# A per-sample term carried in eight extra contraction rows instead of an opening product, with label gathers of eight row counts at the start

## The chip, the cores and the metric

The kernel runs on one core of a Trainium2 chip. The metric is the time of one execution on the device, in microseconds. A run of a kernel beside the kernel before, on one chip, is called a session here. Within a session the executions of one kernel agree to about 0.5%; between sessions they need not, and much of this document is about that. The records of every execution also give the span of the core and the mean clock granted to TensorE. The automatic state label of an execution compares it only with others of the same kernel in its session, so it reads "fast" for everything below; "quick session" and "slow session" are words of this document, defined by the time of the kernel before in that session (11.2 ms or 15.4 to 15.7 ms).

## The reference

For 16,384 samples with 69 items and one label each, rows of an embedding table (96 values) are fetched, combined, weighted by a small network, pooled into ten groups, and passed through a three-layer top.

```python
u = emb[batch_user]                              # 16384 x 69 x 96
ql = emb[batch_label[:, 0]]                      # 16384 x 96
q = jnp.broadcast_to(ql[:, None, :], u.shape)
z = jnp.concatenate([q, u, q - u, q * u], axis=-1)
h = _dice(z @ W1 + b1, a1, EPS_DICE)             # "first product"
att = (h @ W2 + b2) @ W3 + b3
pre = jnp.where((batch_user < ITEM_NUM)[..., None], u * att, 0.0)
pooled = jnp.einsum('gf,bfe->bge', window, pre)
# ... three dense layers on [pooled, ql]
```

Split by the four parts of z, `z @ W1 + b1` is `u (W1b - W1c) + (q*u) W1d + c`, with `c = q (W1a + W1c) + b1`. The term c is the same for all 69 items of a sample. The change is about how c gets into the sum.

## The kernel before

The samples go in 32 blocks of 512, a block in 69 chunks of 512 items, and two chunks make a "pair", the step of the main loop. A main chunk holds 8 samples with 64 items each; the 5 remaining items of each sample make 5 tail chunks. Per chunk GpSimd issues four gathers of 128 rows, TensorE transposes them, ScalarE and VectorE copy them out as `uT` and `quT`, and the first product accumulates two parts in a PSUM bank:

```python
def seed(i):                                  # opens the bank of a pair with c
    ph = ps_h.tile([P, 512], F32, tag="h", ...)
    nc.tensor.matmul(ph, zrow[:, 0:P], zrow, start=True, stop=False)   # zeros, bf16
    ...
    nc.scalar.copy(ph.rearrange("h (s f) -> h s f", f=FM),
                   by_field(cs[n0][0][:, k0 * NS : (k0 + 1) * NS]))    # c, per sample
def hidden(i, ph, uT, quT):
    for w, x, last in [(A, uT, False), (Wp, quT, True)]:
        for j in range(2):
            nc.tensor.matmul(ph[j * H1 : (j + 1) * H1, :], w, x[:, j, :], start=False, stop=last)
```

The label rows of a block are needed once, at its head, and come two ways. The first block's are gathered by GpSimd. Those of the other 31 blocks are loaded one row at a time on the SyncE queue, 512 rows a block, each with its row number in a register:

```python
for i, row in enumerate(at):                  # 32 rows per step of the main loop
    nc.sync.dma_start(out=qs[n][p + i : p + i + 1, k, :], in_=emb[bass.ds(row, 1), :])
...
for part in range(BLK // NLD):                # 16 steps, from 31 pairs before the block
    at(first - 31 + part, lambda n=n, part=part: head_gather(n, part))
at(first - 11, lambda n=n: head_turn(n, qs.pop(n)))      # transpose them
```

## Time and profile before

| kernel before | value |
|---|---|
| timed runs, median of 3 | 15,685.73 us (15,658.17 to 15,687.8) |
| the profiled execution | 11,178.86 us, clock 0.707 |
| TensorE / GpSimd / ScalarE / VectorE busy | 87% / 75% / 34% / 29% |
| gathers | 8832, one per 1.256 us |

```profile
1272.55 0.24 SPq L449 DMA_DIRECT2D out<-res  x1
1278.32 120.70 SPq L260 DMA_DIRECT2D q<-in_emb  x224
...
1404.58 156.49 SPq L260 DMA_DIRECT2D q<-in_emb  x288
1613.10 0.23 SPq L449 DMA_DIRECT2D out<-res  x1
```

The queue then stands still until the result of an earlier block is there to be sent; a view of its waits says the same (us in total, times, longest).

A block of the main loop lasts 342 us. So the queue is at work for over 80% of the time even in a quick session, and what it waits for is the progress of the rest.

### The profile page before, as it was taken

To read this page: it belongs to the slowest core of one execution; us is meant where nothing else is said; L and a number is where in the kernel's file an instruction comes from. 1 tells how busy PE (TensorE), PEld (TensorE's weight loads), DVE (VectorE), ACT (ScalarE), POOL (GpSimd) and SP (SyncE) were. 2 spreads that over 40 slices of the span, in tenths; PEclk is the share of its full clock that TensorE was granted. 3 is DMA by queue.
4 is the path that set the end of the run, shared out by engine and by line. 5 is a ranking of instruction groups with operands and counts; after the bars stand their busy time and mean duration, and the time that the engine had idled before them with its cause. 6 is when DMAs were issued, how large, how long until landed. Compare 5 with 4: busy or idle time off the path is not lost.

```text
span 11177.1 us, 157529 instructions
## 1 busy us (share of the span) xinstructions
PE 9700.5 (87%) x41348; PEld 4721.0 (42%) x41348; DVE 3187.3 (29%) x5424; ACT 3760.0 (34%) x6086; POOL 8404.8 (75%) x8842
## 2 busy tenths in 40 slices
PE   6888888888888898888888888888888888988888
PEld 3444444444444444444444444444444344444444
DVE  2222222222222222222222222222222222222222
ACT  2333333333333333333333333333333333333332
POOL 7777777777777777777777777777777777777775
PEclk6767677677776767767777667776677776677767
DMA  2222222222222222222222222222222222222221
GB/s 45 41 41 41 41 41 41 41 41 41 41 41 41 41 41 41 41 42 41 41 41 41 41 41 41 40 41 42 41 41 41 41 42 41 41 41 41 41 40 29
DMA packets 323169, 456.81 MB, mean 41 GB/s; under 512 B 175712, under 2 KB 180864, under 8 KB 322272
## 3 DMA queue, kind: packets, MB, share of 16 engines
q0 software_dynamic: 282752, 434.87, 19.6%
q1 hardware_dynamic: 37886, 10.92, 0.5%
q8 instruction: 333, 5.46, 0.2%
q14 instruction: 564, 4.62, 0.1%
q10 hardware_dynamic: 1634, 0.94, 0.0%
HBM read 446.04 MB, written 0.07 MB: 40 GB/s over the span
## 4 chain that ended last, share of the span: by engine, by line
PE 33%; POOL 32%; issue 16%; DMA 10%; SPq 5%; ACT 2%; DVE 1%; POOLq 0%; ACTq 0%
POOL u L229 32%; PE ph L343 12%; DMA u<-in_emb,rows 10%; PE acc L393 9%; PE p L423 4%; SPq L260 3%; PE ptr L325 3%; PE prow L354 2%; SPq L252 2%; PE ph L295 2%; PE pa L363 1%; ACT y L346 1%; DVE y L347 1%; ACT y L345 1%; PE patt L370 1%
## 5 line engine op out<-in xcount | busy, mean ns | idle before, releaser
L229 POOL DMA_INDIRECT u<-in_emb,rows x8832 | 8400.1, 951 | 2692.9 <-issue 2459.0
L325 PE MATMUL ptr<-ident,u 128*96 128x128 f32 x8832 | 2006.4, 353 | 1189.5 <-DMA u<-in_emb,rows 1172.1
L325 PEld LDWEIGHTS ptr<-ident,u 128*96 128x96 f32 x8832 | 1221.0, 155 | 3053.7 <-DMA u<-in_emb,rows 1526.9
L393 PEld LDWEIGHTS acc<-rw,u 128*96 128x96 f32 x16384 | 2048.5, 217 | 531.8 <-issue 531.2
L393 PE MATMUL acc<-rw,u 128*96 128x20 f32 x16384 | 2160.4, 282 | 1.8 <-DVE rw L376 1.3
L336 ACT COPY uT<-ptr 96x512 f32<-96x512 f32 x2208 | 1283.4, 581 | 2207.0 <-DVE quT L328 2039.4
L347 DVE TENSOR_TENSOR y<-ph,y 128x512 f32<-128x512 f32 x1104 | 763.5, 692 | 4394.8 <-ACT y L346 4292.3
L345 ACT ACTIVATE y<-ph 128x512 f32<-128x512 f32 x1104 | 659.1, 597 | 3754.1 <-PE ph L343 3753.9
L343 PE MATMUL ph<-uT,A 96*64 96x512 f32 x4416 | 1793.5, 904 | 0.0
L343 PE MATMUL ph<-quT,w 96*64 96x512 f32 x4416 | 1671.9, 847 | 0.0
L328 DVE TENSOR_TENSOR quT<-ptr,qT 96x512 f32<-96x512 f32 x2048 | 1348.9, 679 | 611.5 <-PE ptr L325 607.0
L402 DVE COPY pooled<-acc 96x160 f32<-96x160 f32 x1008 | 433.3, 430 | 2189.9 <-PE acc L393 2184.4
L346 ACT ACTIVATE y<-y,a1c,na1c 128x512 f32<-128x512 f32 x1104 | 897.2, 813 | 36.6
L343 PEld LDWEIGHTS ph<-quT,w 96*64 96x64 f32 x4416 | 442.8, 194 | 1074.9 <-issue 1074.9
L298 ACT COPY ph<-cT 128x512 f32<-128x512 f32 x1008 | 591.3, 587 | 498.2 <-PE ph L295 497.8
L295 PE MATMUL ph<-zrow 1*128 1x512 bf16 x1104 | 527.6, 478 | 193.4 <-DVE y L347 191.7
L423 PE MATMUL p<-pooled,wf 96*100 96x512 f32 x1280 | 659.4, 660 | 1.2 <-DVE x L427 0.8
L343 PEld LDWEIGHTS ph<-uT,A 96*64 96x64 f32 x4416 | 282.6, 177 | 550.0 <-issue 464.8
L354 PE MATMUL prow<-y,v 128*32 128x512 f32 x2208 | 455.2, 909 | 0.0
L356 ACT COPY row<-prow 128x512 f32<-128x512 f32 x276 | 161.5, 585 | 628.4 <-PE prow L354 622.9
L423 PEld LDWEIGHTS p<-pooled,wf 96*100 96x100 f32 x1280 | 232.2, 190 | 287.7 <-issue 285.5
L423 PE MATMUL p<-pre,V 96*100 96x512 f32 x640 | 314.6, 625 | 0.0
(71 smaller groups left out, 2318.5 us busy)
## 6 DMA issues: line engine op xcount, KB each, us to landing
q<-in_emb SPq DMA_DIRECT2D x15872, 0.4 KB
u<-in_emb,rows POOLq DMA_INDIRECT x8832
ids<-in_idx SPq DMA_DIRECT2D x32, 140.0 KB
wf<-in_Wf ACTq DMA_DIRECT2D x1, 825.0 KB
out<-res SPq DMA_DIRECT2D x32, 2.0 KB
w<-in_W SPq DMA_DIRECT2D x1, 96.0 KB
q<-in_emb,ids POOLq DMA_INDIRECT x4
wf<-in_Wf ACTq DMA_DIRECT2D x1, 62.5 KB
```

The lines of the kernel that those rows point to most:

```text
L229: nc.gpsimd.indirect_dma_start(out=dst, out_offset=None, in_=emb, in_offset=bass.IndirectOffsetOnAxis(ap=index, axis=0),)
L295: nc.tensor.matmul(ph, zrow[:, 0:P], zrow, start=True, stop=False)
L325: nc.tensor.transpose(ptr[:, t * P : (t + 1) * P], u[:, 4 * j + t, :], ident)
L328: nc.vector.tensor_tensor(quT[:, j, :].rearrange("e (s f) -> e s f", f=FM), ptr.rearrange("e (s f) -> e s f", f=FM), by_field(q[:, k * NS ...
L336: nc.scalar.copy(uT[:, j, :], ptr)
L343: nc.tensor.matmul(ph[j * H1 : (j + 1) * H1, :], w, x[:, j, :], start=False, stop=last)
L345: nc.scalar.activation(y, ph, AF.Sigmoid, scale=S_DICE)
L346: nc.scalar.activation(y, y, AF.Identity, bias=a1c, scale=na1c)
L347: nc.vector.tensor_mul(y, ph, y)
L354: nc.tensor.matmul(pr[32 * k : 32 * (k + 1), :], v2, y, start=True, stop=True)
L393: nc.tensor.matmul(pa[:, j, 2 * t : 2 * t + 2, :].rearrange("e n g -> e (n g)"), u[:, 4 * j + t, :], rw[:, i % 4, j, t, :], start=True, st ...
L423: nc.tensor.matmul(p1, w[:, h * DH : (h + 1) * DH], x, start=(k == 0), stop=(k == KTOP - 1))
```

## The change

Its intent: drop the opening product and ScalarE's copy of c. The stationary matrix A gets eight more rows, the c of the chunk's 8 samples, and the moving matrix `uT` gets eight constant rows that pick the sample of each column. Then the first product's contraction over 104 rows adds c by itself. As A now holds c, there are two halves of A for a block (32 chunks each), refilled by small transfers. In addition the first block's label tiles are each gathered with two smaller row counts before the full 128.

```diff
@@ constants
-    A = const.tile([E, H1], F32, name="A")
-    nc.vector.tensor_sub(A, w1[:, 1, :], w1[:, 2, :])
+    A = [const.tile([E + NS, HM, H1], F32, name=f"A{h}") for h in range(2)]
+    ...
+    uTs = [const.tile([E + NS, 2, 512], F32, name=f"uT{i}") for i in range(5)]   # rows 96.. one-hot by sample
@@ first_head
-        for k in range(NQ):
-            gather(q[:, k, :], ids[0][:, NT + k : NT + k + 1])
+        for k, part in enumerate([(127, 126), (125, 124), (122, 120), (119, 112)]):
+            for m in (*part, P):
+                gather(q[0:m, k, :], ids[0][0:m, NT + k : NT + k + 1])
@@ head_row and seed go; in their place
+    def head_rows(n):
+        c = bpool.tile([P, NQ, H1], F32, tag="c", name=f"c{n}")
+        pc = ps_x.tile([P, NQ, H1], F32, tag="x", name=f"pc{n}")
+        for k in range(NQ):
+            nc.tensor.matmul(pc[:, k, :], qTs[n % 2][:, k * P : (k + 1) * P], Cq, start=True, stop=True)
+        nc.scalar.copy(c, pc)
+        return c
+    def head_weights(c, h):
+        for s in range(NS):
+            for k in range(NQ // 2):
+                nc.sync.dma_start(
+                    out=A[h][E + s : E + s + 1, k * HM // 2 : (k + 1) * HM // 2, :],
+                    in_=c[s::NS, h * NQ // 2 + k, :],
+                )
@@ hidden
+                nc.tensor.matmul(p, A[k // HM][:, k % HM, :], uT[:, j, :], start=True, stop=False)
@@ plan of a block
+            at(first - 7, lambda n=n: head_weights(cs[n], 0))
+            at(first + 4, lambda n=n: head_weights(cs.pop(n), 1))
```

Left out: bookkeeping, the tail chunks (which take c from a product of their own with Cq), and smaller buffer edits.

More of the change, by code (lines that the diff above doesn't have):

```diff
@@ L31 @@
 F32 = mybir.dt.float32
-BF16 = mybir.dt.bfloat16
 I32 = mybir.dt.int32
@@ L50 @@
 NMAIN = BLK // NS
+HM = NMAIN // 2
 NCH = NMAIN + NTAIL
@@ L94, in rec_kernel @@
     upool = ctx.enter_context(tc.tile_pool(name="upool", bufs=14))
-    tpool = ctx.enter_context(tc.tile_pool(name="tpool", bufs=5))
+    tpool = ctx.enter_context(tc.tile_pool(name="tpool", bufs=4))
     hpool = ctx.enter_context(tc.tile_pool(name="hpool", bufs=3))
@@ L107, in map_ids, with by_field @@
     def map_ids(n, ids):
-        rows = ipool.tile([P, NT], I32, tag="rows", name=f"rows{n}")
-        nc.vector.scalar_tensor_tensor(rows, ids[:, 0:NT], float(ITEM_NUM), ids[:, 0:NT], ALU.is_ge, ALU.add)
-        return rows
+        rows = ids[:, 0:NT]
+        nc.vector.scalar_tensor_tensor(rows, rows, float(ITEM_NUM), rows, ALU.is_ge, ALU.add)
+        return rows
+    def by_field(ap):
+        return ap.rearrange("e (s o) -> e s o", o=1).to_broadcast([ap.shape[0], NS, FM])
     ids, rows = {0: load_ids(0)}, {}
@@ L121, in rec_kernel @@
     nc.sync.dma_start(out=w1, in_=W1.rearrange("(k e) h -> e k h", e=E))
-    Cq = const.tile([E + 1, 2, H1], F32, name="Cq")
-    for i in range(2):
-        nc.vector.tensor_add(Cq[0:E, i, :], w1[:, 0, :], w1[:, 2, :])
-    nc.sync.dma_start(
-        out=Cq[E : E + 1], in_=b1.rearrange("(o q h) -> o q h", o=1, q=1).to_broadcast([1, 2, H1])
-    )
-    Wp = w1[:, 3, :]
-    A = const.tile([E, H1], F32, name="A")
-    nc.vector.tensor_sub(A, w1[:, 1, :], w1[:, 2, :])
+    Cq = const.tile([E + 1, H1], F32, name="Cq")
+    nc.vector.tensor_add(Cq[0:E], w1[:, 0, :], w1[:, 2, :])
+    nc.sync.dma_start(out=Cq[E : E + 1], in_=b1.rearrange("(o h) -> o h", o=1))
+    Wp = w1[:, 3, :]
+    A = [const.tile([E + NS, HM, H1], F32, name=f"A{h}") for h in range(2)]
+    nc.vector.tensor_sub(A[0][0:E, 0, :], w1[:, 1, :], w1[:, 2, :])
+    for h in range(2):
+        nc.vector.tensor_copy(
+            A[h][0:E, 1 - h :, :], A[0][0:E, 0:1, :].to_broadcast([E, HM - 1 + h, H1])
+        )
+    uTs = [const.tile([E + NS, 2, 512], F32, name=f"uT{i}") for i in range(5)]
+    for t in uTs:
+        for j in range(2):
+            nc.vector.tensor_copy(
+                t[E : E + NS, j, :].rearrange("e (s f) -> e s f", f=FM), by_field(ident[E : E + NS, E : E + NS])
+            )
     qTs = []
     for i in range(2):
-        t = const.tile([E + 1, BLK + NS], F32, name=f"qT{i}")
-        nc.vector.memset(t[:, BLK:], 0.0)
+        t = const.tile([E + 1, BLK], F32, name=f"qT{i}")
         nc.vector.memset(t[E : E + 1, :], 1.0)
@@ L197, in rec_kernel @@
     nc.vector.tensor_scalar_mul(sbf2, bf2c, S_BN)
-    zrow = const.tile([1, 512], BF16, name="zrow")
-    nc.vector.memset(zrow, 0.0)
     with tc.tile_pool(name="prep_ps", bufs=1, space=PSUM) as pps:
@@ L266, in head_turn @@
         nc.vector.tensor_copy(qTs[n % 2][0:E, 0:BLK], pq)
-    def head_row(n):
-        cT = bpool.tile([P, BLK], F32, tag="cT", name=f"cT{n}")
-        pc = ps_x.tile([P, BLK], F32, tag="x", name=f"pc{n}")
-        for i in range(2):
-            nc.tensor.matmul(
-                pc[i * H1 : (i + 1) * H1, :],
-                Cq[:, i, :],
-                qTs[n % 2][:, i * NS : i * NS + BLK],
-                start=True,
-                stop=True,
-            )
-        nc.scalar.copy(cT, pc)
-        cU = bpool.tile([P, BLK], F32, tag="cU", name=f"cU{n}")
-        pc = ps_x.tile([P, BLK], F32, tag="x", name=f"pc2_{n}")
-        nc.tensor.matmul(pc, Cq.rearrange("e i h -> e (i h)"), qTs[n % 2][:, 0:BLK], start=True, stop=True)
-        nc.scalar.copy(cU, pc)
-        return cT, cU
@@ L288, in by_field @@
-    def by_field(ap):
-        return ap.rearrange("e (s o) -> e s o", o=1).to_broadcast([ap.shape[0], NS, FM])
-    def seed(i):
-        ph = ps_h.tile([P, 512], F32, tag="h", name=f"ph{i}")
-        nc.tensor.matmul(ph, zrow[:, 0:P], zrow, start=True, stop=False)
-        (n0, k0), (n1, k1) = chunk(2 * i), chunk(2 * i + 1)
-        if n0 == n1 and k1 < NMAIN:
-            nc.scalar.copy(
-                ph.rearrange("h (s f) -> h s f", f=FM), by_field(cs[n0][0][:, k0 * NS : (k0 + 1) * NS])
-            )
-        elif n0 == n1 and k0 >= NMAIN:
-            nc.scalar.copy(ph, cs[n0][1])
-        else:
-            for j, (n, k) in enumerate([(n0, k0), (n1, k1)]):
-                lo, hi = j * H1, (j + 1) * H1
-                if k < NMAIN:
-                    nc.scalar.copy(
-                        ph[lo:hi].rearrange("h (s f) -> h s f", f=FM),
-                        by_field(cs[n][1][lo:hi, k * NS : (k + 1) * NS]),
-                    )
-                else:
-                    nc.scalar.copy(ph[lo:hi], cs[n][1][lo:hi, :])
-        return ph
+    def head_rows(n):
[5 more added lines that the diff above has]
+        return c
@@ L315, in fetch @@
+    def head_weights(c, h):
[4 more added lines that the diff above has]
+                    in_=c[s::NS, h * NQ // 2 + k, :],
+                )
     def fetch(i):
         u = upool.tile([P, 8, E], F32, tag="u", name=f"u{i}")
-        uT = tpool.tile([E, 2, 512], F32, tag="uT", name=f"uT{i}")
+        uT = uTs[i % len(uTs)]
         quT = tpool.tile([E, 2, 512], F32, tag="quT", name=f"quT{i}")
@@ L335, in fetch, with hidden @@
                 nc.vector.tensor_tensor(quT[:, j, :], ptr, q[:, 0:BLK], ALU.mult)
-            nc.scalar.copy(uT[:, j, :], ptr)
+            nc.scalar.copy(uT[0:E, j, :], ptr)
         return u, uT, quT
-    def hidden(i, ph, uT, quT):
-        for w, x, last in [(A, uT, False), (Wp, quT, True)]:
-            for j in range(2):
-                nc.tensor.matmul(ph[j * H1 : (j + 1) * H1, :], w, x[:, j, :], start=False, stop=last)
+    def hidden(i, uT, quT):
+        ph = ps_h.tile([P, 512], F32, tag="h", name=f"ph{i}")
+        places = [chunk(2 * i + j) for j in range(2)]
+        sums = [ph[j * H1 : (j + 1) * H1, :] for j in range(2)]
+        for (n, k), p in zip(places, sums):
+            if k >= NMAIN:
+                nc.tensor.matmul(p, Cq, qTs[n % 2], start=True, stop=False)
+        for j, ((n, k), p) in enumerate(zip(places, sums)):
+            if k < NMAIN:
+                nc.tensor.matmul(p, A[k // HM][:, k % HM, :], uT[:, j, :], start=True, stop=False)
+            else:
+                nc.tensor.matmul(p, A[0][0:E, 0, :], uT[0:E, j, :], start=False, stop=False)
+        for j, p in enumerate(sums):
+            nc.tensor.matmul(p, Wp, quT[:, j, :], start=False, stop=True)
         y = ypool.tile([P, 512], F32, tag="y", name=f"y{i}")
@@ L363, in attend_tail @@
         nc.tensor.matmul(pa, vrep[j * H1 : (j + 1) * H1, :], y[j * H1 : (j + 1) * H1, :], start=True, stop=True)
-        nc.vector.scalar_tensor_tensor(pres[n][:, k - NMAIN, :], pa, bb[0:E], uT[:, j, :], ALU.add, ALU.mult)
+        nc.vector.scalar_tensor_tensor(pres[n][:, k - NMAIN, :], pa, bb[0:E], uT[0:E, j, :], ALU.add, ALU.mult)
     def spread(b, row):
@@ L446, in top3 @@
         nc.tensor.matmul(p3, wf3, x2, start=True, stop=True)
-        res = xpool.tile([1, BLK], F32, tag="res", name=f"res{n}")
+        res = xpool.tile([DH, BLK], F32, tag="g1", name=f"res{n}")[0:1]
         nc.vector.tensor_scalar(res, p3, bf3c, None, ALU.add)
@@ L451, in rec_kernel @@
     out_v = out.rearrange("(n b) o -> n (o b)", n=NBLK)
-    cs, pooled, pres, x1s, x2s, qs, us, hs, phs, ys, bands, rws, p1s = ({} for _ in range(13))
+    cs, pooled, pres, x1s, x2s, qs, us, hs, ys, bands, rws, p1s = ({} for _ in range(12))
     def top_steps(n):
@@ L481, in rec_kernel @@
             at(first - 11, lambda n=n: head_turn(n, qs.pop(n)))
-            at(first - 9, lambda n=n: cs.__setitem__(n, head_row(n)))
+            at(first - 9, lambda n=n: cs.__setitem__(n, head_rows(n)))
+            at(first - 7, lambda n=n: head_weights(cs[n], 0))
+            at(first + 4, lambda n=n: head_weights(cs.pop(n), 1))
         for s, work in enumerate(top_steps(n)):
@@ L489, in rec_kernel @@
         head_turn(0, first_head())
-        cs[0] = head_row(0)
+        cs[0] = head_rows(0)
+        for h in range(2):
+            head_weights(cs[0], h)
         for i in range(NPAIR + POOL_LAG + 16):
-            if 0 <= i - 1 < NPAIR:
-                phs[i - 1] = seed(i - 1)
             if 0 <= i - POOL_LAG < NPAIR:
@@ L513, in rec_kernel @@
             if 0 <= i - 2 < NPAIR:
-                ys[i - 2] = hidden(i - 2, phs.pop(i - 2), *hs[i - 2])
+                ys[i - 2] = hidden(i - 2, *hs[i - 2])
             if i < NPAIR:
@@ L535 @@
     tail = user[:, :, FM:].reshape(NBLK, NQ, P, NTAIL).transpose(0, 2, 3, 1).reshape(NBLK, P, NTAIL * NQ)
+    labels = x["batch_label"].reshape(NBLK, NQ, P).transpose(0, 2, 1)
     window = x["window"]
@@ L539 @@
         wtile[n, :, n, :] = window[:, :FM].T
-    labels = x["batch_label"].reshape(NBLK, NQ, P).transpose(0, 2, 1)
     arrays = {
```

## The prediction

> **What bounds the kernel now.** I read the page's totals first, then the groups of the GpSimd line, then that line's waits, then the queue view, then a stretch of the timeline.
>
> ```profile
> span 11177.1 us, 157529 instructions
> PE 9700.5 (87%) x41348; PEld 4721.0 (42%) x41348; DVE 3187.3 (29%) x5424; ACT 3760.0 (34%) x6086; POOL 8404.8 (75%) x8842
> ...
> L229 POOL DMA_INDIRECT u<-in_emb,rows x8832 | 8400.1, 951 | 2692.9 <-issue 2459.0
> L295 PE MATMUL ph<-zrow 1*128 1x512 bf16 x1104 | 527.6, 478 | 193.4 <-DVE y L347 191.7
> ```
>
> TensorE looks like the bound at 87%, and it is not. GpSimd is busy for 75%, but its idle time is nearly all "issue", time in which it waited for nothing: 8400.1 + 2692.9 = 11093.0 us of 11177.1. The answer for the gather's line says how regular that is:
>
> ```profile
> L229 POOL DMA_INDIRECT u<-in_emb,rows x8832: 940/944/1582, 8.6 to 11100.4; - x197
> ...
>   issue: 2459.9, 8068
>   PE ptr L325: 105.8, 347
>   DMA u<-in_emb,rows: 101.9, 334
> ```
>
> The first of the 8832 starts at 8.6 us and the last at 11100.4, so one per (11100.4 - 8.6) / 8831 = 1.256 us from beginning to end, 0.944 at work and 0.30 of issue. The few waits put down to others are also 0.30 us each (105.8 / 347), so they are the same issue time under another name. The timeline in the middle of the run:
>
> ```profile
> 5000.06 0.94 POOL L229 DMA_INDIRECT u<-in_emb,rows  x1 [0.30 <-issue]
> 5001.31 0.94 POOL L229 DMA_INDIRECT u<-in_emb,rows  x1 [0.30 <-issue]
> 5002.56 0.94 POOL L229 DMA_INDIRECT u<-in_emb,rows  x1 [0.31 <-issue]
> 5003.80 0.94 POOL L229 DMA_INDIRECT u<-in_emb,rows  x1 [0.30 <-issue]
> ```
>
> Gathers start every 1.25 us while TensorE works in bursts around them. The profiled execution is bound by GpSimd's issue of gathers, and by nothing else; the chain of waits agrees, with 32% on the gather and 16% on "issue".
>
> The main fact stands outside the profile. The timed runs take 15,658 to 15,688 us, the profiled one 11,179: 1.40 times as long, with 0.2% between the runs. There are 8836 gathers (8832 plus four of labels). If they are the bound in both, one costs 15685.73 / 8836 = 1.775 us in the timed runs against 1.256 here, 0.52 us more, or 4 ns for each of 128 rows. So the gather seems to have a fast state, which the profile caught, and a slow one, which the timed runs sit in. That the same instruction can be slower is visible: the longest of the 8832 took 1582 ns. What selects the state no view of this profile shows. I choose to hang the prediction on it.
>
> **What the Trainium skill says.** "GPSIMD Engine Reference", section "When to use GPSIMD", says that descriptors of a gather are made in software by a pair of GpSimd's cores. The trace agrees in that the gather occupies GpSimd for 944 ns and the data moves elsewhere. "DMA: Bandwidth & Descriptors", section "Why a DMA increments its semaphore by 16 and not by 1", says that a transfer runs on the largest number k of engines, up to 16, that divides its slowest dimension (127 partitions give 1), and that for software descriptors a k under 16 starts at a round-robin cursor. In the queue view:
>
> ```profile
> q0 software_dynamic: 282752, 434.87, 19.6%
> ```
>
> 282752 packets are 32 per gather (8836 x 32), which fits 16 engines with one data packet and one semaphore packet each; every gather of before has 128 rows. By the page's rule the eight new counts 127, 126, 125, 124, 122, 120, 119, 112 would give k = 1, 14, 5, 4, 2, 15, 7, 16: eight different values, 64 in all, so the cursor ends where it began. No run here shows that yet. "TensorE: Matmul & The Clock Gate", section "LDWEIGHTS (loading the stationary operand)", says that a weight load's time goes with columns and not with the contraction dimension. The trace shows the same of a product: four products over 97 rows take as long as four over 96.
>
> ```profile
> 14.08 1.98 PE L273 MATMUL pc<-qT,Cq 97*64 97x512 f32 x4 [1.73 <-DVE qT L266]
> ...
> 30.68 1.98 PE L343 MATMUL ph<-uT,A 96*64 96x512 f32 x4
> ```
>
> **The change part by part.** (1) No opening product. Each pair loses the bf16 product that opens the PSUM bank, 1104 x 478 ns = 528 us of TensorE, and up to 192 us of its waits for VectorE's last read of that bank. (2) ScalarE loses the copy of c into PSUM: 1008 x 587 ns = 591 us, some 650 with the pairs of the tail fields and the block edges. (3) Eight more rows in the first product: nothing, by the 97 against 96 rows above. (4) The 5 tail chunks of 69 have c from a product of their own: 32 x 5 = 160 products at 1793.5 / 4416 = 0.41 us of covered time each, +65 us. (5) Per block, three 512-column products and two copies become four 64-column products and one copy: some 50 us less of TensorE and 20 of ScalarE. TensorE's sum: 9700 - 528 + 65 - 50 = about 9190 us, 82% of the same span. (6) The SyncE queue gets 32 small transfers per block, 1024 in all, at about 0.42 us of issue (the start of the timeline shows 0.40 to 0.45 for one) = 430 us over the run. It sends 15,872 single label rows now, 224 of them in 120.66 us at the start, 0.54 us each, so about 8.6 ms plus 0.4 of 11.2. It stays under the span, but it now waits for c and for the weights' readers, and the labels queue behind that; the next block's labels may come a step or two late. GpSimd can run about six pairs ahead of TensorE (14 buffers against a pooling lag of 8), so this should not stop the gathers. (7) The label tiles: 4 gathers become 12. Eight extra at 1.25 us are 10 us, plus some waits for the earlier write to the same tile, in all 10 to 30 us once. The copies that fill the new constants are VectorE work under the same run-ahead.
>
> None of (1) to (6) lies on the path of the profiled execution. The tail after the last gather is 11177.1 - 11100.4 = 77 us; two or three pairs in it get about a microsecond shorter each. So in a fast state I expect 11,179 + 20 - 5 = about 11,195 us. In a slow state, 15,686 + 20 = about 15,705.
>
> **The rivals.** *First: the redundant gathers bring the fast state.* Each of the eight is overwritten at once by the full gather, so it does nothing for the result; somebody wrote it for its effect on GpSimd. Code that makes descriptors in a loop over rows, or over k engines, may have a state that depends on the shapes it has seen. For it: [...]the runs are tight, and the profile proves that the fast state exists. Against it: the profile reached the fast state with 128-row gathers alone, so the counts are not needed there, and they need not suffice elsewhere. Time: about 11,195.
>
> *Second: the state has to do with being timed or profiled, and the counts don't touch it.* Then GpSimd still bounds, all of TensorE's saving is hidden, and the time is about 15,700. The chain of the profiled run shows nothing against this.
>
> *Third: the timed runs are bound by TensorE at a low clock.* The granted clock was 0.707 in the mean, and the clock row alternates between 6 and 7 tenths. If it stayed at half, the busy time would be up to 9700 x 0.707 / 0.5 = 13,716 us, and with the 1477 us of idle near 15,200, not far from 15,686. Then (1) to (5) count: 510 x 1.41 = 720 us, giving some 15,000. Against it: [...]in the profile no gather waited long for it, even in slices at 0.6.
>
> *Fourth: the SyncE queue becomes the bound.* Its 9.0 ms have 20% of room in the fast state and more in the slow one. If the late labels stopped gathers for two steps of 10 us in each of 31 blocks, +620 us at most, 11,800.
>
> **Range and chances.** I give the first rival 0.67, the second 0.21, the third 0.07, other outcomes 0.05. The two main outcomes lie 4500 us apart, so no narrow range holds 8 times in 10; it has to run from a little under the fast estimate to a little over the slow one. The point is the likelier outcome, about 11,190. Faster by over 2% needs less than 15,372: first and third rival and part of the rest, 0.75. Within 2%: the second, 0.22. Slower: 0.03.
>
> **What would show each step.** If the profile of the changed kernel has its gathers at about 944 ns every 1.25 us and a span near 11.2 ms, TensorE near 82% and no wait of the gather longer than its issue, steps (1) to (7) are right, whatever the timed runs say. If its timed runs are near its profile, the first rival is right; if they are at 15.7 ms, the second. A timed 15.0 ms speaks for the third. New long waits of the label transposes for their transfers, with gathers waiting behind them, would show the fourth. I am wrong on the whole if gathers take a third duration, or if the clock falls so far with the lighter load that TensorE holds up gathers.

## More of the kernel before

The prediction shows what GpSimd does in this profile. The view that it does not show turned out to matter: the timeline of the SyncE queue of the kernel before, over two blocks (start in us, length, engine, line, operation, how many).

A block's 512 label rows take this queue from 1278.32 to 1561.07, 283 us.

```profile
SPq L449 <- DVE res L448: 2230.6, 31, 350.3
```

The profiled execution and the timed ones are 40% apart. To judge by the times, the profile is of a quick session and the timed runs are of a slow one, which I did not know.

## The result and the profile after

The changed kernel took 17,409.25 us (median of 4 runs, 17,394.99 to 17,417.38), beside 15,686.76 us for the kernel before (median of 4). The ratio is 1.1099, with an interval of 1.108 to 1.1118. Ratios here are the mean time of one kernel's fast runs over that of the other's of the same rounds, so not quite the ratio of the medians quoted. The prediction's own figure for a slow state was about 15,705.

The page of the changed kernel, whose profiled execution took 17,404.9 us: its totals and two of its groups (busy us, mean ns, idle before, and what ended most of it).

```profile
span 17404.9 us, 156797 instructions
...
PE 8991.9 (52%) x40628; PEld 4628.6 (27%) x40628; DVE 3098.9 (18%) x5432; ACT 3130.6 (18%) x4918; POOL 8392.8 (48%) x8850
...
L239 POOL DMA_INDIRECT u<-in_emb,ids x8832 | 8377.0, 948 | 8888.4 <-PE acc L385 4716.9
...
L276 PE MATMUL pq<-ident,q 128*96 128x128 f32 x128 | 41.4, 365 | 3464.0 <-DMA q<-in_emb 2441.1
```

This one is a slow session, profile and times both. A gather is no slower: 948 ns in the mean, against 951 before. GpSimd stands idle for half of the time, and of that 4716.9 us end with TensorE's pooling products, which free the buffer the gather writes. TensorE in turn stood still for 3464 us at the transposes of the label rows, `pq`, most of it until the label rows had landed. What the gather waited for, with its durations (minimum, median, maximum in ns) in the first line:

```profile
L239 POOL DMA_INDIRECT u<-in_emb,ids x8832: 938/945/1596, 40.0 to 17304.2; - x197
...
  PE acc L385: 4716.9, 147
  issue: 2204.3, 7217
```

So the label rows are late, then TensorE, then GpSimd. Why they are late is in the SyncE queue's timeline, here over one block:

```profile
2263.49 34.80 SPq L271 DMA_DIRECT2D q<-in_emb  x32
2298.71 38.96 SPq L292 DMA_DIRECT2D A<-c  x16
2346.08 188.82 SPq L271 DMA_DIRECT2D q<-in_emb  x192
...
2540.40 209.12 SPq L271 DMA_DIRECT2D q<-in_emb  x288
2749.62 0.24 SPq L441 DMA_DIRECT2D out<-res  x1
2776.99 86.60 SPq L292 DMA_DIRECT2D A<-c  x32
```

The 512 rows now take 486 us in this block, instead of 283, with the transfers `A<-c` of the change in between. After the first of the 31 blocks the mean is 454.0 us from the first to the last row of a block, and 87.3 us from there to the next block's first row, 541.3 us in all. Such a sum equals a block in any steady kernel. What marks the queue as the pace is that it no longer stands still for the results of earlier blocks: 30 of the 32 results are sent 0.1 us after the transfer before them, where in the quick profile of before 31 had to be waited for. The three largest waits of the new transfers on that queue, and the one for a result:

```profile
SPq L292 <- remote: 1070.0, 15, 93.7
SPq L292 <- ACT c L285: 540.1, 20, 28.1
SPq L292 <- PE ph L331: 390.9, 10, 66.6
...
SPq L441 <- DVE res L440: 180.3, 1, 180.3
```

All the transfers' waits but those for other transfers come to 2,475 us, 77 us a block. Where the trace names what ended them, it is mostly the computing of c, or a product of TensorE, as the readers of the half of A to be overwritten are; for 1070.0 us ("remote") it names nothing, since many semaphore records are missing (see "What stays open"). The transfers' own issue takes another 601.8 us, 0.59 us each. In a queue served in order, the next label rows stand behind all this.

There are two causes in this, and they must be kept apart. One is the change's transfers on the queue. The other is that the queue is slower in itself: in every second block no transfer stands among the rows, and these still take 413 to 436 us, where the quick profile of before has 283. A row load is two register instructions and the transfer; the duration of the second register instruction, over all 15,872 rows (minimum, median, maximum in ns), first in the kernel before in its quick session, then in the changed kernel in its slow one:

```profile
L260 SPq MOVE q<-in_emb x15872: 29/29/38, 16.9 to 10571.0; - x199
```

```profile
L271 SPq MOVE q<-in_emb x15872: 1/29/1414, 82.1 to 16851.2; - x199
```

The median is the same and the maximum is 37 times as long. In the slow trace 1,416 of these moves take over 600 ns, most of them about 0.7 us and some about 1.4; in no quick trace does one. Counted by what GpSimd does at the time, they take 163 ns in the mean in stretches of 5 us of which gathers fill over 60%, and 31 ns in stretches without a gather. TensorE is held too. Its timeline in the slow trace shows pooling products, first held one by one, then running freely (the bracket is the idle time before).

```profile
1262.00 0.19 PE L385 MATMUL acc<-rw,u 128*96 128x20 f32 x1 [2.64 <-issue]
1265.50 0.19 PE L385 MATMUL acc<-rw,u 128*96 128x20 f32 x1 [3.30 <-issue]
1267.60 0.19 PE L385 MATMUL acc<-rw,u 128*96 128x20 f32 x1 [1.91 <-issue]
...
1289.74 1.46 PE L385 MATMUL acc<-rw,u 128*96 128x20 f32 x16
```

Sixteen such products took 1.46 us in the second place, and three took 5.8 us in the first, with nothing that the profile shows them waiting for.

### The profile page after: what moved, and what is told of

It is laid out like the page before. It is cut to its first block, busy times and chain, and to the rows that moved or that the text cites. A ratio compares the mean times of both kernels' runs of the same rounds, so it can differ in the third digit from the quotient of the medians.

```text
span 17404.9 us, 156797 instructions
## 1 busy us (share of the span) xinstructions
PE 8991.9 (52%) x40628; PEld 4628.6 (27%) x40628; DVE 3098.9 (18%) x5432; ACT 3130.6 (18%) x4918; POOL 8392.8 (48%) x8850
## 5 line engine op out<-in xcount | busy, mean ns | idle before, releaser
L239 POOL DMA_INDIRECT u<-in_emb,ids x8832 | 8377.0, 948 | 8888.4 <-PE acc L385 4716.9
L385 PE MATMUL acc<-rw,u 128*96 128x20 f32 x16384 | 2052.7, 270 | 2916.4 <-issue 1508.8
L307 PE MATMUL ptr<-ident,u 128*96 128x128 f32 x8832 | 1572.9, 324 | 812.4 <-issue 542.8
L335 PE MATMUL ph<-quT,w 96*64 96x512 f32 x4416 | 1767.8, 800 | 177.7 <-issue 170.2
L276 PE MATMUL pq<-ident,q 128*96 128x128 f32 x128 | 41.4, 365 | 3464.0 <-DMA q<-in_emb 2441.1
L331 PE MATMUL ph<-uT,A 104*64 104x512 f32 x4096 | 1710.2, 850 | 109.9 <-issue 108.8
L307 PEld LDWEIGHTS ptr<-ident,u 128*96 128x96 f32 x8832 | 1132.0, 148 | 2192.8 <-issue 1654.9
L346 PE MATMUL prow<-y,v 128*32 128x512 f32 x2208 | 640.9, 862 | 302.4 <-issue 157.4
L331 PEld LDWEIGHTS ph<-uT,A 104*64 104x64 f32 x4096 | 286.1, 169 | 664.5 <-issue 645.6
L362 PE MATMUL patt<-ident,row 128*128 128x128 f32 x1104 | 246.2, 350 | 217.9 <-issue 132.0
```

What stands on the lines that cost most here:

```text
L239: nc.gpsimd.indirect_dma_start(out=dst, out_offset=None, in_=emb, in_offset=bass.IndirectOffsetOnAxis(ap=index, axis=0),)
L307: nc.tensor.transpose(ptr[:, t * P : (t + 1) * P], u[:, 4 * j + t, :], ident)
L331: nc.tensor.matmul(p, A[k // HM][:, k % HM, :], uT[:, j, :], start=True, stop=False)
L335: nc.tensor.matmul(p, Wp, quT[:, j, :], start=False, stop=True)
L346: nc.tensor.matmul(pr[32 * k : 32 * (k + 1), :], v2, y, start=True, stop=True)
L385: nc.tensor.matmul(pa[:, j, 2 * t : 2 * t + 2, :].rearrange("e n g -> e (n g)"), u[:, 4 * j + t, :], rw[:, i % 4, j, t, :], start=True, st ...
```

## The experiments

There were twelve sessions and eighteen runs. The kernel before was run in each session, and it sorts them:

| sessions | chip | kernel before, us |
|---|---|---|
| 9 quick | 14 (three times), 11 (twice), 4, 12, 1, 3 | 11,179 to 11,209 |
| 3 slow | 15, 7, 2 | 15,439; 15,509; 15,644 |

No session held both states, and no chip was seen in both. The pair on record (15,687 and 17,409) belongs with the slow ones.

The theory to test first was mine (T1): a gather has a slow state, and the eight row counts change it. Its rivals were that the slow time is the label queue's doing (T2) and that the state comes with the chip or session whatever the kernel (T3).

### The parts alone, on chip 14

**b0**: the kernel before, unchanged.

> The kernel before, unchanged, for a profile of its slow executions. My recorded theory of a slow gather (T1) expects gathers of about 1.47 us and one per 1.775 us from beginning to end. The rival (T2, label rows): gathers of 0.94 us as in the profile on hand, every 1.25 us while they run, with long pauses once per block, because the 512 single label rows of a block take SyncE about 490 us (15,686 / 32) in place of 283 us. A third (T3): it takes 11.2 ms here, and the two states of before come and go by execution.

Measured: 11,184.92 us beside 11,178.54, ratio 1.0004. The kernel that had taken 15,686 us took 11,185 here. That shows T3's half of the matter: the time of one and the same kernel differs by a factor of 1.40 from session to session.

**b_counts**: the kernel before with the eight row counts alone.

```diff
-        for k in range(NQ):
-            gather(q[:, k, :], ids[0][:, NT + k : NT + k + 1])
+        for k, part in enumerate([(127, 126), (125, 124), (122, 120), (119, 112)]):
+            for m in (*part, P):
+                gather(q[0:m, k, :], ids[0][0:m, NT + k : NT + k + 1])
```

> The kernel before with only the label tiles of the first block gathered with the eight other row counts first. If the row counts bring a fast state: 11.2 ms. If they bring the slow state of the changed kernel: above 15.7 ms, up to 17.4. If they have no lasting effect (T2): 15.69 plus 0.03 ms, within 1% of the kernel before, label rows at the same pace.

Measured: 11,217.73 us, ratio 1.0034 (1.0004 to 1.0063). In a quick session the counts cost about 0.3%.

**a_plain**: the changed kernel with that edit undone.

> The changed kernel with the four plain label gathers of before. If the row counts cause the 11%: 15.7 ms or less. If they have no lasting effect (T2, the loss is from the 32 weight transfers per block that stand among the label rows on SyncE): 17.4 ms less 0.03.

Measured: 11,210.16 us, ratio 1.0027 (0.9998 to 1.0056), clock 0.753.

**a_pool**: the changed kernel with all label rows gathered on GpSimd, four gathers a block, so that no label row goes through SyncE.

```diff
-            for part in range(BLK // NLD):
-                at(first - 31 + part, lambda n=n, part=part: head_gather(n, part))
+            at(first - 20, lambda n=n: head_pool(n))   # 4 x gather(qs[n][:, k, :], ids[n][:, NT + k : NT + k + 1])
```

> The changed kernel, the labels of blocks 1 to 31 gathered on GpSimd, four gathers per block, no single rows on SyncE. T2 expects the pauses to go and GpSimd to bind: (8844 + 124) x 1.256 = 11.26 ms, plus 0.1. A theory in which the gathers or TensorE are slow in themselves (T1, or a slow clock) expects it to stay above 15 ms.

Measured: 11,363.61 us, ratio 1.0164. The session was quick, so what the run was made for, the slow state without the label queue, was not seen. It shows the price of that way out: 124 more gathers at 1.25 us are 155 us, and 153 us were measured over a_plain.

### The changed kernel in a quick session

**a0**: the changed kernel, unchanged, three timed runs.

> The changed kernel as it is. In the first call the kernel before took 11.18 ms in every execution, as in its first profile, and 15.69 in none, and the changed kernel without the row counts took 11.21. If the slow executions belong to a chip or a session (T3), this takes about 11.21 + 0.04 = 11.25 ms wherever the kernel before takes 11.18, and 17.4 wherever that takes 15.69. If the row counts put the changed kernel into a slow state (T1 with its sign turned), it takes 17.4 ms beside a kernel before of 11.18.

Measured: 11,232.69 us beside 11,191.12, ratio 1.0039 (1.0016 to 1.0061). The page and the gather's view of this run:

```profile
span 11230.8 us, 156797 instructions
...
PE 8363.6 (74%) x40628; PEld 4273.7 (38%) x40628; DVE 3153.8 (28%) x5432; ACT 3148.1 (28%) x4918; POOL 8421.9 (75%) x8850
```

```profile
L239 POOL DMA_INDIRECT u<-in_emb,ids x8832: 940/945/1606, 40.1 to 11153.3; - x197
...
  issue: 2504.5, 8217
```

The gathers run one per 1.258 us and wait for hardly anything but their issue, although TensorE has 1,337 us less to do. The waits of the new transfers are there on chip 14 too, 1,151 us in all; the two largest entries of the queue's waits:

```profile
SPq L292 <- PE ph L331: 598.6, 31, 36.5
SPq L292 <- ACT c L285: 517.5, 29, 32.6
```

But the label rows of a block take 291.6 us here and 54.1 us pass to the next block's (the first block left out). These 345.7 us are a block of GpSimd's too (276 gathers at 1.258 us, 347 us), and the gathers do not wait: the queue just keeps up. It has little room left. Only the last two of the 32 results are still waited for, 418.9 us in all, where before it was 31 and 2230.6 us, and the page's chain of waits now has 47% on SyncE. So in a quick session the change costs 0.4% and brings nothing.

### A slow label queue made on a quick chip

If T2 is right, a queue that needs longer for its rows must by itself give times like those on record, on a chip in its quick state. Each label row was loaded a second time, into a tile that nobody reads; the results stay right.

**b_twice** is the kernel before with this, **a_twice** the changed one.

```diff
             nc.sync.dma_start(out=qs[n][p + i : p + i + 1, k, :], in_=emb[bass.ds(row, 1), :])
+            nc.sync.dma_start(out=ds[n][p + i : p + i + 1, k, :], in_=emb[bass.ds(row, 1), :])
```

> The kernel before with each label row loaded twice, the second time into a tile that nothing reads: SyncE's work per block rises by 512 x 0.403 us = 206 us, from 283 to 489. The theory that the slow executions are those in which SyncE gets through a block's rows in 490 us (T2) expects 31 x 489 + some 450 at the ends = about 15.6 ms, close to the 15,687 recorded for the kernel before, with gathers of 0.94 us and pauses once per block. A theory in which the slow executions need something else than late labels (a slow gather, a slow TensorE) expects well under 15 ms, since SyncE has 62 us to spare in each block.

> The changed kernel with each label row loaded twice. T2 with the weight transfers on the same queue: 489 us, 15 us for 32 transfers, and 40 to 80 us of waiting for c and for the weights' readers, 544 to 584 us per block, so 17.3 to 18.5 ms, slower than b_twice by 9 to 17%, as the two kernels stood in the recorded times (1.11). If the order of the SyncE queue doesn't matter: within 3% of b_twice.

Measured on chip 4: b_twice 15,942.11 us, a_twice 17,468.51 us, kernel before 11,183.19 us. Both have the size of the times on record, and a_twice over b_twice is 1.0957, where the record has 1.1099. That the sizes come so near is partly chance: doubling gives 493 us for a block's rows, the slow trace of the changed kernel 413 to 436 where no transfer stands among them. The waits of b_twice across all engines have the same pattern as the changed kernel's slow profile, label transposes and then gathers:

```profile
PE pq L267 <- DMA q<-in_emb: 5989.5, 61, 124.6
POOL u L229 <- PE acc L395: 4797.3, 86, 187.6
```

The difference of the two, 1,526 us, can be found on the queue. In b_twice the rows of a block take 492.6 us and the next block's follow after 5.9; in a_twice they take 498.3 and follow after 48.8. The differences, 5.7 and 42.9 us, times 31 blocks are 1,507 us. They are made of the new transfers, which b_twice does not have: their own issue, 1024 at 0.60 us, is 615.5 us, and their waits come to 895.5 us, together 1,511 and nearly the whole of 1,526. The largest waits:

```profile
SPq L294 <- ACT c L287: 523.6, 30, 32.2
...
SPq L294 <- PE ph L333: 335.1, 16, 22.6
```

So this much is shown: where the label queue is the pace, the change costs some 10%, and it does so through that queue. By the queue's own account three fifths of this are its standing still for c and for the readers of A, and two fifths the issue of the transfers, which leaves little for the change's other edits.

**a_twice_act** is a_twice with the new transfers on ScalarE's queue.

```diff
     def head_weights(c, h):
...
-                nc.sync.dma_start(
+                nc.scalar.dma_start(
```

> As a_twice, with the 32 weight transfers per block issued from ScalarE's queue in place of SyncE's. If the loss comes from label rows waiting behind those transfers, it goes: 15.6 ms, within 2% of b_twice. If it comes from the other parts of the change: as a_twice.

Measured: 16,669.01 us. Of the 1,526 us, 799 came back, 52%. The gap between blocks fell to 6.0 us, as in b_twice, but the row loads took longer, 517.1 us, and the queue has a new wait:

```profile
SPq L272 <- DMA A<-c: 428.1, 35, 22.2
```

With the same wait at the second copies (120.9 us) this is 549 of the 727 us that are still lost to b_twice. A label row now waits for a transfer of c that touches none of its memory and is on another queue. I take it that the two share a completion semaphore; no run tests it. Moving the transfers to another queue is thus half a remedy.

**b_pool**: the kernel before with all label rows gathered on GpSimd, as in a_pool.

> The kernel before with the labels of blocks 1 to 31 gathered on GpSimd, no single rows on SyncE. Where the kernel before takes 11.18 ms: 124 more gathers x 1.256 us = 156 us more, 11.34 ms. Where it takes 15.69: T2 (the slow executions are those in which SyncE sends the rows late) expects 11.4 ms all the same; if TensorE's own slow stretches bind there, 13 ms or more.

Measured on chip 12, quick: 11,343.12 us beside 11,183.21, ratio 1.0142, as expected. No label row is on SyncE here, and the time is longer by what 124 more gathers take (160 us, 1.29 us each): in a quick session GpSimd's issue is the pace of the kernel before.

### Runs meant for a slow session, and others

**a_twice_early** starts the rows of a_twice 14 steps earlier, to see whether the size of the lead matters.

```diff
-                at(first - 31 + part, lambda n=n, part=part: head_gather(n, part))
+                at(max(0, first - 45 + part), lambda n=n, part=part: head_gather(n, part))
```

> As a_twice, but the label rows of a block stand 14 steps earlier in the program, so that some 120 us of them stand before the first half of the weight transfers and nearly all before the second. If the loss of a_twice against b_twice (1526 us, 49 us per block) is SyncE standing still until c exists and the weights are read, it shrinks to the 32 transfers' own issue, 13 to 15 us per block: 15,942 + 31 x 15 = 16.4 ms. If the transfers cost it by their data or by TensorE's side of the change, it stays at 17.4 ms.

Measured: 24,459.97 us beside 15,439.42. Two things were mixed. The session was slow, the first caught. And the edit had a fault: the block's item numbers are loaded on the same queue at an unchanged step, so they now came behind all those rows, and VectorE waited 10,763.7 us for them. Nothing follows for the lead. But the trace shows the slow state in a second kernel: 1,749 of 31,744 moves over 600 ns.

**a_pool_2** and **a_pool_3** are a_pool again, in the hope of a slow session.

> The changed kernel without single label rows on SyncE once more, for a call that falls on a chip in the slow state (the call before this one did: the kernel before took 15.44 ms there). On a fast chip: 11.36 ms, as before, and nothing new. On a slow chip: T2 (late label rows are the whole of it) expects about 11.4 ms beside a kernel before of 15.4 to 15.7. If TensorE's slow stretches, which the slow trace also shows, bind by themselves: 13 ms or more.

> The changed kernel without single label rows on SyncE, a third time, again for a chip in the slow state (a_pool_2 fell on a fast one). Fast chip: 11.36 ms. Slow chip: T2 (late label rows are the whole of it) expects about 11.4 ms beside a kernel before of 15.4 to 15.7; if TensorE's slow stretches bind by themselves, 13 ms or more.

Measured: 11,374.81 and 11,376.85 us on chip 11, both quick (ratios 1.0168 and 1.0177). Nothing new.

**a_half**: the changed kernel with half of a block's label rows on GpSimd (two gathers) and half on SyncE.

```diff
-            for part in range(BLK // NLD):
-                at(first - 31 + part, lambda n=n, part=part: head_gather(n, part))
+            for part in range(BLK // NLD // 2):
+                at(first - 23 + part, lambda n=n, part=part: head_gather(n, part))
+            at(first - 20, lambda n=n: head_pool(n))   # gathers for k in range(NQ // 2, NQ)
```

> The changed kernel with half of a block's labels gathered on GpSimd (two more gathers) and half as single rows on SyncE. Fast chip: 11.233 + 31 x 2 x 1.256 us = 11.31 ms. Slow chip, T2: SyncE needs about 245 us per block in place of 490 and keeps up with GpSimd's 349, so 11.3 to 11.6 ms beside a kernel before of 15.4 to 15.7. If TensorE's slow stretches bind there by themselves: 13 ms or more.

Measured on chip 1, quick: 11,325.31 us, ratio 1.0106, as expected. The same kernel again, **a_half_2**:

> The changed kernel with half of the labels gathered on GpSimd, for a chip in the slow state, after b_half took 13.79 ms there beside 15.51 (late label rows gone, TensorE's pauses left). If TensorE's side binds what is left, the changed kernel's saving there (528 us of opening products and their waits for VectorE, 2498 us in the b_half trace) shows: 12.0 to 13.3 ms on a slow chip, faster than both kernels there. If the weight transfers on SyncE still hold it up: 13.8 or more. Fast chip: 11.33 ms as before.

Measured on chip 3, quick: 11,309.68 us, ratio 1.0106.

**b_half**: the kernel before with that edit.

> The kernel before with half of a block's labels gathered on GpSimd. Fast chip: 11.183 + 31 x 2 x 1.256 us = 11.26 ms. Slow chip, T2: SyncE keeps up (about 245 us per block against 348), so 11.3 to 11.6 ms beside a kernel before of 15.4 to 15.7; if TensorE's slow stretches bind by themselves, 13 ms or more.

Measured on chip 7, slow at last: 13,790.24 us beside 15,509.31, ratio 0.8892 (0.8832 to 0.8953). So in a slow session, halving the label queue's work makes the kernel before 11% faster: the late label rows do bind there. But they are not all. With 11,184 us for a quick session, the slow one costs the kernel before 4,325 us, and this edit took 1,719 of them back. The rest is not the queue's, whose largest wait, a view of its own says, is now slack, 3,963.3 us for results of earlier blocks:

```profile
SPq L454 <- DVE res L453: 3963.3, 23, 435.0
```

The chain of waits, as far as the sparse records allow one, gives the larger part to TensorE, and the waits have pauses of TensorE's own and of the opening product:

```profile
PE 57%; another core or an unknown queue 22%; issue 10%; ACT 6%; DVE 4%; POOL 1%; DMA 0%; DVEq 0%; POOLq 0%; ACTq 0%
```

```profile
PEld acc L398 <- issue: 3409.2, 1039, 27.3
...
PE ph L300 <- DVE y L352: 2498.1, 556, 26.8
```

In the quick profile of before the first entry was 531.2 us and the second 191.7. The gathers still take 0.94 us. With the label queue relieved, the held TensorE seems to be the pace at 13.8 ms; no run relieves it to test this.

**a_plain_2** and **a_plain_3** repeat a_plain, the counts left out.

> The changed kernel without the eight row counts, for a chip in the slow state. If the row counts have no lasting effect there either: 1.11 times the kernel before, less 0.03 ms, so 17.0 to 17.4 ms. If they are what costs the 11%: as the kernel before, 15.4 to 15.7. Fast chip: 11.21 ms as before.

> As a_plain_2, again for a chip in the slow state: 17.0 to 17.4 ms there if the row counts have no lasting effect, 15.4 to 15.7 if they cost the 11%. Fast chip: 11.21 ms.

Measured: 11,203.05 us on chip 3 and 11,212.54 on chip 14, both quick, ratios 1.0011 and 1.0022. The changed kernel without the counts was not seen in a slow session. That they neither bring nor prevent the state follows in another way: the slow state was seen without them (the kernel before, b_half) and with them (the changed kernel, a_twice_early), and so was the quick one (b0; a0, b_counts).

**a_twice_order** mends a_twice_early: item numbers first, then the rows, other steps for the two refills of A, and a smaller tile for the second copies (not shown).

```diff
-    ipool = ctx.enter_context(tc.tile_pool(name="ipool", bufs=2))
+    ipool = ctx.enter_context(tc.tile_pool(name="ipool", bufs=3))
...
-            at(first - 24, lambda n=n: ids.__setitem__(n, load_ids(n)))
+            at(max(0, first - 43), lambda n=n: ids.__setitem__(n, load_ids(n)))
-                at(first - 31 + part, ...head_gather(n, part))
+                at(max(0, first - 42 + part), ...head_gather(n, part))
-            at(first - 7, lambda n=n: head_weights(cs[n], 0))
-            at(first + 4, lambda n=n: head_weights(cs.pop(n), 1))
+            at(first - 5, lambda n=n: head_weights(cs[n], 0))
+            at(first, lambda n=n: head_weights(cs.pop(n), 1))
```

> As a_twice, with the order of SyncE's work changed again, without the fault of a_twice_early: the indices of a block are loaded before its label rows (three buffers), two to three parts of the next block's rows stand before the first half of the weight transfers and some eight before the second half, which moves up by four steps. On a fast chip, if the loss of a_twice against b_twice (1526 us) is SyncE standing still until c exists and the weights have been read, the gap of 49 us between the last row of a block and the first of the next goes to 6, the transfers' own 13 to 15 us stay, and the time is 15,942 + 31 x 15 = about 16.4 ms. If other parts of the change cost it: 17.3 or more. On a slow chip: about 22 ms, and nothing of this is told apart.

Measured on chip 2, slow: 23,266.34 us beside 15,644.42. The time has no partner, as b_twice was never in a slow session. The queue's standing still did go: 6.6 us from a block's last row to the next block's first (48.8 in a_twice, 87.3 in the changed kernel on record), and the new transfers' wait for c fell to 26.6 us in the whole run. So the order of the queue can be mended; what that is worth to the changed kernel, without doubled rows, was not measured.

No version beat both kernels. In quick sessions the kernel before is the best (11,179 to 11,209 us). In a slow one b_half is faster than it, at a price in quick ones that was measured on the changed kernel only (a_half, 1.0106).

## Why the prediction was wrong

**The reading of the quick profile held.** "The profiled execution is bound by GpSimd's issue of gathers, and by nothing else": b_pool confirms it, with its 124 more gathers paid in full, and a0, with the gathers at the same pace and TensorE's saving hidden. The estimate for that state was 11,195 us, and a0 took 11,233.

**The step that failed** is the one after it: "If they are the bound in both, one costs 15685.73 / 8836 = 1.775 us in the timed runs". They are not the bound in both. In the slow trace a gather takes 945 ns in the median, as in the quick ones, and GpSimd waits for buffers. I divided a time by a count and took the quotient for a duration that no view showed. "What selects the state no view of this profile shows. I choose to hang the prediction on it" was the choice that put 0.67 on the counts. The runs show instead a state that comes with the session or its chip, which no run tells apart, and in which SyncE and TensorE are held. The first rival fell by the result itself; the counts cost 0.3% and change nothing else in a quick session (b_counts).

**The fourth rival was the right mechanism, with the wrong sign.** I wrote that the queue's "9.0 ms have 20% of room in the fast state and more in the slow one". In the slow state the queue is what is slowed: 454.0 us for a block's rows instead of 283. My sum of 9.0 ms assumed the quick state's durations. With that, step (6), "it stays under the span", fails, and "this should not stop the gathers" with it: 4716.9 us of waits. I had named the wait for c and for the weights' readers and sized its harm at "two steps of 10 us" a block. The wait is 77 us a block, in part in place of the queue's waits for results, and the transfers' own issue 19 us more, 0.59 us each and not 0.42. The cost of the change on record is 1,722 us, or 54 us a block. "at most 11,800" was worked out from the quick state alone. That the queue carries the loss wherever it is the pace is shown by the doubled rows. That it does so in the slow state is read from the changed kernel's trace and from b_half: the slow state has no trace of the kernel before, and the changed kernel was not run there with a relieved queue.

**The second rival** was right that "the counts don't touch it". It was wrong to tie the state to being timed or profiled, as the changed kernel's profile, 17,404.9 us, is in the slow state too, and wrong in "GpSimd still bounds": about 15,700 was expected of it.

**The third rival** was partly right. TensorE seems to bind a part of the slow time, as b_half has it at 13.8 ms, but not by a low clock. The clock of the kernel before was 0.645 to 0.651 on chip 7, where my estimate of that rival needed 0.5; instructions are held between products.

**The smaller terms**, as a0 has them against the profile of before. (1) The opening product is gone, 528 us. (2) ScalarE fell from 3760.0 to 3148.1, 612 us, within the 591 to 670 expected. (3) The 104-row products take 804 ns beside 754 for the 96-row products with quT in the same trace; before, with 96 rows in both, it was 904 beside 847. The ratio is 1.07 both times, so the rows were free. (4) The tail products took 157.6 us and not 65: I counted 160, but the profile lists each such product as two records, so there are 320, at 157.6 / 320 = 0.49 us of covered time. (5) c's products fell from 95.7 to 33.2 us, 62 for 50. TensorE's sum should then be about 9,270 us and it was 8363.6: the granted clock rose from 0.707 to 0.752, and the most frequent products got shorter (transposes from 353 to 321 ns, pooling products from 282 to 263). (7) The label gathers: the first gather of items started at 40.13 us and not at 8.57, 31.5 us later where 10 to 30 were given. The timeline of GpSimd at the start of a0 shows why:

```profile
3.42 2.75 POOL L239 DMA_INDIRECT q<-in_emb,ids  x1 [2.10 <-DMA ids<-in_idx]
11.78 1.04 POOL L239 DMA_INDIRECT q<-in_emb,ids  x1 [5.61 <-DMA q<-in_emb,ids]
```

The first of them, with 127 rows, took 2.75 us and the next had to wait 5.61 us for it to land, as both write the same tile.

**What stays open.** What puts a session into the slow state is not known. The instruction records are sparse there: of the about 17,600 semaphore updates that a quick trace has for a gather's semaphore, the slow ones have 2,477 to 4,951, and the chain of waits of the changed kernel, followed back from the end, breaks off after 4% of the span. Missing records would fit a recording that is congested and holds the engines up, and all times come from recorded executions; but that is only argued. They also make what the slow traces name as the end of a wait less certain. Also open: the changed kernel without the counts, with half or with none of the label rows on SyncE, in a slow session.

## What to carry to other kernels

When the timed runs and the profiled one differ by 40%, the profile does not describe what is timed; put the kernel before on a chip again, next to everything else, before explaining the gap by any one instruction. A queue served in order is an engine like the others: add up its work and its standing still for a block, and ask what it does when its own instructions get slower. Transfers that must wait for fresh results should not stand in front of transfers that others need early.

## What the Trainium skill lacked or had wrong

- No page describes the state in which SyncE's and TensorE's instructions are held, mostly for about 0.7 us at a time; SyncE's mostly in stretches with gathers (a move 163 ns in the mean, 31 without). In it, the longest register move of SyncE went from 38 to 1414 ns, and the kernel before took 15.4 to 15.7 ms where it takes 11.2 (3 of 12 sessions).
- "DMA: Bandwidth & Descriptors", section "Issuing engines are not separate DMA queues", says that the sequencer's time to initiate a DMA is usually small relative to the DMA. The traces have no landing times for the single label rows to compare with, but for a long series of such loads this time is the cost that counts: 0.403 us of SyncE from one row of 384 bytes to the next when nothing holds it, 512 a block, 206 us of a block's 342. Doubling them made the kernel 1.43 times as long (b_twice).
- The same page's section "Why a DMA increments its semaphore by 16 and not by 1" gives the number of engines as the largest divisor up to 16 of the row count. The data packets of a0's gathers fit it for all eight counts, as the prediction worked them out. The rows came in 1 share for 127 rows, 2 equal ones for 122, 4 for 124, 5 for 125, 7 for 119, and 14, 15 and 16 for 126, 120 and 112, in packets of at most 11 rows. The page does not say that the rest of the 16 shares get packets too, of 4 bytes for each row of a share (for 127 rows, 165 packets of 44 bytes and 15 of 24), nor that the gather takes GpSimd the longer the fewer the shares: 2.75 us with 1 (the first gather of its run; before's first, of 128 rows, took 1.16), 1.67 with 2, 1.31 with 4, 1.20 with 5, 1.09 with 7, and 0.96 to 1.04 with 14 to 16.
